# Rows 1 to 3 of a gated attention kernel: the input loaded already transposed, and normalized in that layout

## The chip, the cores and the metric

The kernel runs on one core of one Trainium2 chip. The metric is the device time of one execution in microseconds, the median of the runs: 1109.39 us over three runs (1108.53 to 1110.27) for the kernel before the change. The profile is one execution, recorded instruction by instruction. In what follows, PE or TensorE is the matrix engine, DVE is VectorE, ACT is ScalarE, POOL is GpSimd, and SP is the engine that here issues nearly all of the DMAs. L12 is line 12 of the kernel before.

## The reference

The input x has 4 rows of a batch, 512 tokens each, 1024 features. All of it is float32. Cut to what is computed:

```
xn  = (x - mean(x)) / sqrt(var(x) + 1e-5)              # per token, over the 1024 features
q, k, v = xn @ Wq, xn @ Wk, xn @ Wv                    # 16 heads of 64
q, k = rotary(q), rotary(k)
s   = softmax(causal(q k^T) / 8) v @ Wo
r   = softmax(xn @ gate_w.T)                           # 8 experts
g   = silu((xn * (r @ in_scale)) @ sign(weight).T * (r @ out_scale) + bias)
out = x + s * g
```

The normalization's mean and deviation belong to a token; everything that follows multiplies over features. On this chip a matmul sums over the partitions, so xn is needed with features on the partitions and tokens along the free dimension: transposed, against the way x lies in memory.

## The kernel before, in words

The code calls a row of the batch b (0 to 3). P is 128, E is 1024, S is 512 tokens of a row, NC = 8 is the number of feature chunks of 128, and TPB = 4 is the number of token tiles of 128 in a row. NGRP = 4 is the number of groups of four heads.

The first phase, up to about 800 us, goes through 16 stages (the loop over `groups`), a row's four quarters g = 0 to 3 one after the other. In each stage three kinds of work are woven together in 16 pieces (`interleave`):

- Projections of the current row (`projections`, `project_qk`, `project_v`, L338 and L425). Each product of two matrices is made by seven products of half size instead of eight, with sums of quarters of weights (S forms, `form_w`, L288) and of the input (T forms, `form_x`, L311 and, in the last row, L303). TensorE executes a float32 matmul as two instructions. Its results go through a ring of four PSUM banks of 128x512, and DVE and ACT read them out of it (L352, L358, L387, L389, L446, L451). The T forms of the next row are asked for at the end of a row's last quarter; the next row's first two products use X itself, the next ones T3 and T2.
- Attention of the group before (`attention_pieces`): scores on TensorE (L525), mask and maximum on DVE, exponential on ACT, scaling on POOL (`softmax`, L561), transposition of the probabilities in 32x32 blocks on DVE (`transpose_blocks`, L579) followed by 16 DMAs on SP that put the blocks in place (L589), and the product with the values (`values`, L604), copied out by ACT (L613) and stored to device memory (L617). Rotation (`rotary`) uses ACT (L319, L320), DVE (L321) and POOL (L322, L323).
- Preparation of the next row, which the change touches. In quarter g = 1 the first two token tiles of row b + 1 are loaded (`load_x`, L161) to two buffers. In quarters 2 and 3, two token tiles each: statistics by `layernorm_scales` (L171, L177, the square root on ACT L179), `normalize` (reciprocal L186, then one DVE instruction over 128 tokens x 1024 features, L187), then `transpose_x`: 8 TensorE transposes of 128x128 (L200) in two groups of four, each through one bank of the ring, the first group's bank copied to X by DVE (L204) and the second's by ACT (L206); then the tile of X is stored to device memory as `xn_d` (L210), from which the second phase loads it. The four groups of a stage stand at pieces 7, 8, 13 and 14.

Row 0 is prepared ahead of all this in a short stretch of its own, by the same functions. X has two buffers, so that X of the next row is filled while X of the current row is in use.

The last phase, from about 800 us on, makes the gated feed-forward product and the output projection. The change does not touch its code.

What sets the order: TensorE executes in the order of the program (`manual_schedule`). The order of the instructions on DVE, ACT and POOL and of the DMAs on SP is made when the program is built, by a scheduler that takes the program's order as priority and moves ahead what its own estimates say is ready; `keep_in_program_order` pins single instructions. On the chip each engine's queue is then strictly in that order, and an instruction that waits holds those behind it. Row 0's stretch is in program order on DVE and ACT too.

Of the kernel before, what the change touches and what calls it, by code (L numbers as in the profile page):

```python
# [9 lines left out]
F32 = mybir.dt.float32  # L10
F32R = mybir.dt.float32r
AF = mybir.ActivationFunctionType  # L12
ALU = mybir.AluOpType
# [7 lines left out]
B, S, E = 4, 512, 1024  # L21
H, D = 16, 64
NE = 8
P = 128
NT = B * S
NC = E // P
NPAIR = H // 2
NGRP = NPAIR // 2
TPB = S // P
# [13 lines left out]
def attn_gated_ffn_kernel(  # L43
    ctx: ExitStack,
    tc: tile.TileContext,
    x: bass.AP,
    wqk: bass.AP,
    wv: bass.AP,
    wo: bass.AP,
# [9 lines left out]
    nc = tc.nc  # L59
# [4 lines left out]
    st = ctx.enter_context(tc.tile_pool(name="stats", bufs=4))  # L64
    sgp = ctx.enter_context(tc.tile_pool(name="sign", bufs=1))
    dp = ctx.enter_context(tc.tile_pool(name="spill", bufs=1, space=DRAM))
# [6 lines left out]
        out=mask,  # L73
        in_=mask,
# [22 lines left out]
    for sign, base in ((1, 0), (-1, 7)):  # L97
        nc.gpsimd.affine_select(
            out=high,
            in_=high,  # L100
# [10 lines left out]
    xn_d = dp.tile([B, TPB, P, E], F32, name="xn_d")  # L111
    at_d = dp.tile([B, TPB, P, E], F32, name="at_d")

    rt_d = dp.tile([B, TPB, 32, P], F32, name="rt_d")

    sg = {n: sgp.tile([P, E], F32R, name=f"sg{n}") for n in range(NC - 1)}
# [4 lines left out]
    xp = ctx.enter_context(tc.tile_pool(name="xn", bufs=2))  # L121
# [26 lines left out]
    def tp_bank(name):  # L148
        return bank(name).rearrange("p (t q) -> p t q", t=TPB)


    X, xin = {}, {}
# [3 lines left out]
    def load_x(b, t):  # L156
        if b == 0:
            xt = X1[:, t, :]
        else:
            xt = xip.tile([P, E], F32, tag="x", name=f"x_{b}_{t}")  # L160
        nc.sync.dma_start(out=xt, in_=x[(b * TPB + t) * P : (b * TPB + t + 1) * P, :])  # L161
        xin[b, t] = xt

    BN, MV = {}, {}

    def half_statistics(b, t, j):
        if j == 0:
            BN[b, t] = st.tile([P, 2, 6], F32, tag="bn", name=f"bn_{b}_{t}")

        tc.keep_in_program_order(  # L170
            nc.vector.bn_stats(BN[b, t][:, j, :], xin[b, t][:, j * HALF : (j + 1) * HALF])  # L171
        )

    def deviation(b, t):
        stats = BN[b, t]
        mv = st.tile([P, 2], F32, tag="mv", name=f"mv_{b}_{t}")
        nc.vector.bn_aggr(mv, stats)  # L177
        std = st.tile([P, 1], F32, tag="std", name=f"std_{b}_{t}")
        nc.scalar.activation(std, mv[:, 1:2], AF.Sqrt, bias=eps)  # L179
        MV[b, t] = mv, std  # L180

    def normalize(b, t):
        xt = xin[b, t]
        mv, std = MV[b, t]
        rstd = st.tile([P, 1], F32, tag="rstd", name=f"rstd_{b}_{t}")
        nc.vector.reciprocal(rstd, std)  # L186
        nc.vector.tensor_scalar(xt, xt, mv[:, 0:1], rstd, op0=ALU.subtract, op1=ALU.mult)  # L187

    def layernorm_scales(b, t):
        half_statistics(b, t, 0)  # L190
        half_statistics(b, t, 1)
        deviation(b, t)

    def transpose_x(b, t, g):
        if b not in X:
            X[b] = xp.tile([P, NC, S], F32, tag="X", name=f"X_{b}")
        tp = tp_bank(f"xtp_{b}_{t}_{g}")
        for j in range(4):
            c = 4 * g + j
            nc.tensor.transpose(tp[:, j, :], xin[b, t][:, c * P : (c + 1) * P], ident)  # L200
        dst = X[b][:, 4 * g : 4 * g + 4, t * P : (t + 1) * P]

        if (g == 0 and b > 0) or (g == 1 and (b, t) == (0, TPB - 1)):
            nc.vector.tensor_copy(dst, tp)  # L204
        else:
            nc.scalar.copy(dst, tp)  # L206
        if g == 1:

            queue = nc.scalar if (b, t) == (B - 1, TPB - 1) else nc.sync
            queue.dma_start(  # L210
                out=xn_d[b, t].rearrange("p (c q) -> p c q", c=NC),
                in_=X[b][:, :, t * P : (t + 1) * P],
            )
# [469 lines left out]
    def load_scales(src):  # L683
        v = xip.tile([P, E], F32, tag="x", name="scales")
        nc.sync.dma_start(out=v, in_=src)
        scales.append(v)

    def split_scales(dst):
        v = scales.pop(0)
        h, low, sign = (row_kind[:, n : n + 1] for n in range(3))  # L690
        pin = tc.keep_in_program_order
        if not scales_done:
            pin(nc.vector.tensor_reduce(h, high, AX.X, ALU.max))
            pin(nc.vector.tensor_scalar(low, h, -1.0, 1.0, op0=ALU.mult, op1=ALU.add))
            pin(nc.vector.tensor_scalar(sign, h, 2.0, -1.0, op0=ALU.mult, op1=ALU.add))
        scales_done.append(dst)

        pin(nc.vector.tensor_copy(dst, v))
        pin(nc.vector.tensor_scalar(v, v, low, None, op0=ALU.mult))
        pin(  # L700
            nc.vector.scalar_tensor_tensor(
                dst, dst.bitcast(F32), sign, v, op0=ALU.mult, op1=ALU.add
            )
        )
# [141 lines left out]
    def attention_pieces(k, late):  # L846

        units = [(*groups[k], i) for i in range(2)]
        w, v = late
        u0, u1 = units  # L850

        def values_and_scores(before, u):
            def both():
                if before:
                    values(before)
                scores(u)
                softmax(u, 1, 3)

            return both

        pieces = [[] for _ in range(16)]

        last = k == len(groups) - 2
        plan = {
            2: lambda: v and transpose_blocks(v),
            3 if last else 4: values_and_scores(w, u0),
            4 if last else 6: lambda: softmax(u0, 2, 0),
            8 if last else 9: lambda: transpose_blocks(u0),  # L870
            9 if last else 12: values_and_scores(v, u1),
            10 if last else 14: lambda: softmax(u1, 2, 0),
        }
        if last:
            plan[14] = lambda: transpose_blocks(u1, ordered=True)
        for n, piece in plan.items():
            pieces[n].append(piece)
        return pieces, units
# [11 lines left out]
    for k, (b, g) in enumerate(groups):  # L890
        pieces = [[] for _ in range(9)]
        if k > 0:
            pieces, late = attention_pieces(k - 1, late)

        def at(n, piece):
            pieces[n].append(piece)


        if g == 0:
            routing = [lambda n=n: router(b, n) for n in range(3)]  # L900
            if k == 0:
                at(0, routing[0])
                at(1, lambda: (load_scales(in_scale), load_scales(out_scale)))
                at(2, routing[1])
                at(4, routing[2])
                at(5, lambda: split_scales(isc))
            else:
                if b < B - 1:
                    at(5, routing[0])
                at(8, routing[1])  # L910
                at(15, routing[2])
        elif g == 1 and b + 1 < B:

            at(11, lambda: [load_x(b + 1, t) for t in range(2)])
            if b == 0:
                at(1, lambda: split_scales(osc))
        elif g > 1 and b + 1 < B:
            t0 = 2 * (g - 2)

            layernorm_scales(b + 1, t0)  # L920
            layernorm_scales(b + 1, t0 + 1)
            normalize(b + 1, t0)
            at(3, lambda: normalize(b + 1, t0 + 1))
            for n, t, h in ((7, t0, 0), (8, t0, 1), (13, t0 + 1, 0), (14, t0 + 1, 1)):
                at(n, lambda t=t, h=h: transpose_x(b + 1, t, h))
            if g == 2:
                at(11, lambda: load_x(b + 1, 2))
                at(15, lambda: load_x(b + 1, 3))
        if k in (5, 9, 12, 14):
            n = {5: 0, 9: 2, 12: 4, 14: 6}[k]  # L930
            at(0, lambda: (load_sign(n), load_sign(n + 1)))
            at(8, lambda: make_sign(n))
            at(15, lambda: make_sign(n + 1))
        if b == B - 1:

            if g < 2:
                load_xn(g)
            if g in (1, 2):
                at(1, lambda: in_scales(g - 1, score_banks))
            if g == 3:  # L940
                z_place[0] = [xip.tile([P, E], F32, tag="x", name=f"z0_{i}") for i in range(2)]
                at(1, lambda: out_scales(0, score_banks))
        if k == 11:

            at(15, lambda: router(b + 1, 0))
        interleave(pieces, fill, 3 * 7 * 4 if k else 3 * 7 * 4 - 8)
        if g == NGRP - 1:
            for _ in fill:
                pass
            if b + 1 < B:  # L950
                for n in (3, 1, 2, 4) if b + 1 < B - 1 else (3, 2, 4, 1):
                    form_x(b + 1, n)
                fill = projections(b + 1)
# [98 lines left out]
    w, v = late  # L1052
# [374 lines left out]
```

## Time and profile before

| | |
|---|---|
| median of 3 runs | 1109.39 us (1108.53 to 1110.27) |
| span of the profiled execution | 1108.7 us; the page gives no other time for it, so it stands 0.7 us under the median |
| TensorE clock granted | 0.996 of full speed |
| DVE, ACT, POOL busy | 79%, 42%, 47% |
| transposes of x (L200) | 128, of which 96 are for rows 1 to 3 |
| DMA traffic | 163.88 MB, 109 GB/s of HBM over the span |
| row 0's projections begin | about 12 us |
| row 1's, 2's, 3's projections begin | about 194, 387 and 584 us |

How to read it: the busy share of TensorE counts each matmul from start to end though they overlap, so the cost of a TensorE step is read from the start times. A timeline line gives the start in us, the length in us, engine, line, operation, result <- operands, shape and count of merged instructions; in brackets, where there are any, the idle time before it and what ended it. A line of the table of stages gives the stretch, its length, the busy time of each engine with its number of instructions, the granted clock, the share of the DMA engines and GB/s.

### The profile page before, as it was taken

The numbers are of one execution on the slowest core, as the hardware profiler recorded it, in microseconds if no ns is written. First come the engines' busy times: TensorE is split into PE (matmuls) and PEld (weight loads), VectorE is DVE, ScalarE is ACT, GpSimd is POOL, SyncE is SP. The second block draws the span as 40 slices with busy tenths as digits, with TensorE's granted clock in tenths as the row PEclk, the third lists the DMA queues.
The fourth block names the chain that finished last, engine by engine and source line by source line (L and its number), as shares of the span: only waits on it lengthen the run. The fifth ranks groups of instructions, "written<-read, shape, count | busy, mean of one in ns | idle before, by whom it ended". The sixth has DMA issues, their size and how long they took to land. (4 is left out here: it accounts for less than half of the span.)

```text
span 1108.7 us, 15895 instructions
## 1 busy us (share of the span) xinstructions
PE 1087.4 (98%) x5176; PEld 790.2 (71%) x5176; DVE 870.4 (79%) x1740; ACT 461.3 (42%) x1072; POOL 518.9 (47%) x566
## 2 busy tenths in 40 slices
PE   9999999999999999999999999999999999999997
PEld 8887778777777877777788687777664545654663
DVE  7888888788988978888887887887776877567663
ACT  2452754453375445427544452655530223122220
POOL 0772645555264555526453562675552433432334
PEclk9999999999999999999999999999999999999999
DMA  9415566544556654455666445544664222431331
GB/s 323 135 69 147 149 184 189 160 137 119 166 155 187 190 154 135 121 163 158 184 183 219 140 148 142 153 125 122 179 193 171 90 93 102 148 119 54 136 114 57
DMA packets 86770, 163.88 MB, mean 148 GB/s; under 512 B 13472, under 2 KB 49056, under 8 KB 80672
## 3 DMA queue, kind: packets, MB, share of 16 engines
q1 hardware_dynamic: 80144, 152.25, 46.1%
q0 software_dynamic: 4832, 9.05, 2.4%
q10 hardware_dynamic: 1712, 1.57, 0.5%
q8 instruction: 41, 0.67, 0.3%
q14 instruction: 41, 0.34, 0.1%
HBM read 95.45 MB, written 25.43 MB: 109 GB/s over the span
## 5 line engine op out<-in xcount | busy, mean ns | idle before, releaser
L561 POOL TENSOR_SCALAR p<-p,rs 128x256 f32<-128x256 f32 (+3 forms) x256 | 183.7, 734 | 200.6 <-DVE rs L559 136.2
L551 ACT ACTIVATE p<-sc,nmx 128x256 f32<-128x256 f32 (+3 forms) x256 | 132.9, 529 | 104.8 <-DVE nmx L548 87.2
L338 PE MATMUL pj<-X,w 128*128 128x256 f32 x576 | 134.3, 382 | 1.7 <-ACT p L551 1.5
L338 PE MATMUL pj<-T,S 128*128 128x256 f32 x512 | 120.5, 385 | 8.5 <-ACT v L613 8.5
L579 DVE STREAM_TRANSPOSE y<-p 128x256 f32<-128x256 f32 x320 | 112.4, 409 | 18.3 <-POOL p L561 16.9
L322 POOL TENSOR_TENSOR sw<-sw,sin_sb 128x512 f32<-128x512 f32 x64 | 85.1, 1330 | 81.1 <-ACT sw L320 75.4
L338 PEld LDWEIGHTS pj<-X,w 128*128 128x128 f32 x576 | 108.1, 190 | 20.0 <-issue 2.9
L338 PEld LDWEIGHTS pj<-T,S 128*128 128x128 f32 x512 | 96.7, 192 | 24.8 <-ACT v L613 11.3
L319 ACT ACTIVATE sw<-c 32x512 f32<-32x512 f32 x128 | 80.3, 628 | 70.0 <-DVE c L352 68.2
L338 PE MATMUL pj<-T,w 128*128 128x256 f32 x448 | 106.6, 382 | 0.0
L548 DVE TENSOR_REDUCE nmx<-sc 128x1 f32<-128x256 f32 (+3 forms) x160 | 105.2, 683 | 1.3
L425 PE MATMUL pj<-w,X 128*128 128x256 f32 x416 | 94.6, 380 | 0.8 <-ACT p L551 0.5
L338 PEld LDWEIGHTS pj<-T,w 128*128 128x128 f32 x448 | 83.4, 190 | 15.5 <-issue 4.6
L323 POOL TENSOR_TENSOR rot<-rot,sw 128x512 f32<-128x512 f32 x64 | 90.8, 1419 | 5.0
L425 PEld LDWEIGHTS pj<-w,X 128*128 128x128 f32 x416 | 78.2, 190 | 12.7 <-ACT p L551 2.0
L545 DVE TENSOR_TENSOR sc<-sc,mask 128x256 f32<-128x256 f32 (+1 forms) x160 | 57.0, 371 | 35.3 <-PE sc L525 35.3
L320 ACT ACTIVATE sw<-c 32x512 f32<-32x512 f32 x128 | 80.4, 628 | 1.6
L425 PE MATMUL pj<-w,T 128*128 128x256 f32 x352 | 80.2, 381 | 0.0
L525 PE MATMUL sc<-rot,rot 64*128 64x128 f32 (+3 forms) x512 | 79.7, 443 | 0.3 <-DVE v L451 0.3
L604 PE MATMUL pv<-p,v 128*64 128x256 f32 (+3 forms) x512 | 76.0, 439 | 0.4 <-issue 0.4
L388 POOL TENSOR_TENSOR part<-part,part 128x256 f32<-128x256 f32 x32 | 24.7, 771 | 105.2 <-ACT part L387 102.0
L613 ACT COPY v<-pv 128x512 f32<-128x512 f32 x32 | 18.7, 585 | 131.5 <-PE pv L604 131.4
(177 smaller groups left out, 1956.9 us busy)
## 6 DMA issues: line engine op xcount, KB each, us to landing
p<-y SPq DMA_DIRECT2D x496, 80.0 KB, 2.1
w<-in_wqk SPq DMA_DIRECT2D x31, 1024.0 KB, 5.3
w<-in_wv SPq DMA_DIRECT2D x16, 1024.0 KB, 5.2
x<-in_x SPq DMA_DIRECT2D x16, 512.0 KB, 4.3
at_d<-v SPq DMA_DIRECT2D x32, 256.0 KB, 2.7
xp<-xn_d SPq DMA_DIRECT2D x16, 512.0 KB, 4.6
ap<-at_d SPq DMA_DIRECT2D x16, 512.0 KB, 5.1
xr<-in_x SPq DMA_DIRECT2D x32, 256.0 KB, 3.0
```

The lines of the kernel that those rows point to most:

```text
L319: nc.scalar.activation(sw[r : r + 32, :], c[r + 32 : r + 64, :], AF.Copy, scale=sc)
L320: nc.scalar.activation(sw[r + 32 : r + 64, :], c[r : r + 32, :], AF.Copy, scale=sc)
L322: nc.gpsimd.tensor_tensor(sw, sw, sin_sb, op=ALU.mult)
L323: nc.gpsimd.tensor_tensor(rot, rot, sw, op=ALU.add)
L338: nc.tensor.matmul(ps, lhsT=wq[:, k, :], rhs=xq[:, k, :], start=(k == 0), stop=(k == 3))
L425: nc.tensor.matmul(ps[:, j, :], lhsT=xq[:, k, j * P : (j + 1) * P], rhs=wq[:, k, :], start=(k == 0), stop=(k == 3),)
L525: nc.tensor.matmul(head(i, h), lhsT=Q[u][r : r + D, i * P : (i + 1) * P], rhs=K[u][r : r + D, : (i + 1) * P], start=True, stop=True,)
L548: nc.vector.tensor_reduce(nmx[:, hs], v, AX.X, ALU.max, negate=True)
L551: nc.scalar.activation(pt[:, h, :], ps[h], AF.Exp, bias=nmx[:, h : h + 1], accum_out=ssum[:, h : h + 1],)
L561: nc.gpsimd.tensor_scalar(pt[:, h, :], pt[:, h, :], rs[:, h : h + 1], 1.0, op0=ALU.mult, op1=ALU.mult,)
L579: nc.vector.transpose(out[:, :, :, o : o + 32], src.rearrange("p h (b c) -> p h b c", b=4))
L604: nc.tensor.matmul(by_block[r : r + D, :, 32 * j :], lhsT=V[u][:, j, r : r + D], rhs=PT[u][:, :, o : o + 32 * (TPB - j)], start=(j == 0), ...
```

## The change

A second copy of the input comes in, `xT`, laid out on the host with the features on the partitions: for each row, 128 partitions x (8 chunks x 512 tokens). For rows 1 to 3 it is loaded straight to X with four DMAs of 512 KB (`load_xT`, two at piece 9 and two at piece 15 of quarter 1). x itself is still loaded by token tiles for the statistics, but is no longer normalized nor transposed there. Instead, the mean and the reciprocal of the deviation of 128 tokens, two numbers on each partition, are written to a small tensor in device memory (`sv_d`, at the end of `layernorm_scales`) and read back as one line of 256 numbers broadcast to all partitions (`load_rows`, one buffer); then POOL subtracts the mean and DVE multiplies by the reciprocal, each as one instruction over 128 partitions x 8 chunks x 128 tokens, in place in X (`normalize_columns`), and the tile is stored to `xn_d` as before. The broadcast loads stand at pieces 3 and 9 of quarters 2 and 3, the normalizations at 6 and 12. Row 0 keeps the transposes; its code loses only the cases that were for the other rows. The store of row 3's last tile, which ACT's queue issued, goes to SP's.

```diff
+    sv_d = dp.tile([B, TPB, 2, P], F32, name="sv_d")
...
+    def load_xT(b, n):
+        if n == 0:
+            X[b] = xp.tile([P, NC, S], F32, tag="X", name=f"X_{b}")
+        for c in range(4 * n, 4 * n + 4, 2):
+            nc.sync.dma_start(
+                out=X[b][:, c : c + 2, :].rearrange("p c q -> p (c q)"),
+                in_=xT[b][:, c * S : (c + 2) * S],
+            )
+
     def layernorm_scales(b, t):
+
         half_statistics(b, t, 0)
         half_statistics(b, t, 1)
         deviation(b, t)
+        mv, std = MV[b, t]
+        nc.vector.reciprocal(mv[:, 1:2], std)
+        with nc.allow_non_contiguous_dma(reason="two numbers per token"):
+            nc.sync.dma_start(out=sv_d[b, t].rearrange("r p -> p r"), in_=mv)
+
+    ROW = {}
+
+    def load_rows(b, t):
+        ROW[b, t] = st.tile([P, 2, P], F32, tag="row", name=f"row_{b}_{t}", bufs=1)
+        nc.sync.dma_start(
+            out=ROW[b, t].rearrange("p r q -> p (r q)"),
+            in_=sv_d[b, t].rearrange("r q -> (r q)")[None, :].to_broadcast((P, 2 * P)),
+        )
+
+    def normalize_columns(b, t):
+        v = X[b][:, :, t * P : (t + 1) * P]
+        mean, rstd = (ROW[b, t][:, r, None, :].to_broadcast((P, NC, P)) for r in range(2))
+        nc.gpsimd.tensor_tensor(v, v, mean, op=ALU.subtract)
+        nc.vector.tensor_tensor(v, v, rstd, op=ALU.mult)
+        nc.sync.dma_start(out=xn_d[b, t].rearrange("p (c q) -> p c q", c=NC), in_=v)
...
         elif g == 1 and b + 1 < B:
 
+            at(9, lambda: load_xT(b + 1, 0))
             at(11, lambda: [load_x(b + 1, t) for t in range(2)])
+            at(15, lambda: load_xT(b + 1, 1))
...
             layernorm_scales(b + 1, t0)
             layernorm_scales(b + 1, t0 + 1)
-            normalize(b + 1, t0)
-            at(3, lambda: normalize(b + 1, t0 + 1))
-            for n, t, h in ((7, t0, 0), (8, t0, 1), (13, t0 + 1, 0), (14, t0 + 1, 1)):
-                at(n, lambda t=t, h=h: transpose_x(b + 1, t, h))
+            for n, t in ((3, t0), (9, t0 + 1)):
+                at(n, lambda t=t: load_rows(b + 1, t))
+                at(n + 3, lambda t=t: normalize_columns(b + 1, t))
```

More of the change, by code (lines that the diff above doesn't have):

```diff
@@ L46, in attn_gated_ffn_kernel @@
     x: bass.AP,
+    xT: bass.AP,
     wqk: bass.AP,
@@ L201, in transpose_x @@
         dst = X[b][:, 4 * g : 4 * g + 4, t * P : (t + 1) * P]
-        if (g == 0 and b > 0) or (g == 1 and (b, t) == (0, TPB - 1)):
+        if g == 1 and t == TPB - 1:
             nc.vector.tensor_copy(dst, tp)
@@ L207, in transpose_x @@
         if g == 1:
-            queue = nc.scalar if (b, t) == (B - 1, TPB - 1) else nc.sync
-            queue.dma_start(
+            nc.sync.dma_start(
                 out=xn_d[b, t].rearrange("p (c q) -> p c q", c=NC),
@@ L1405 @@
         "x": np.ascontiguousarray(a["hidden_states"].reshape(NT, E)),
+        "xT": np.ascontiguousarray(
+            a["hidden_states"].reshape(B, S, NC, P).transpose(0, 3, 2, 1).reshape(B, P, NC * S)
+        ),
         "wqk": np.ascontiguousarray(np.stack([by_group(a["Wq"]), by_group(a["Wk"])], axis=1)),
```

## The prediction

> **What bounds the kernel now.** I read the page's busy row first, then the TensorE timeline around the step that goes, then the busy table of the six stages that hold it (the last two quarters of rows 0, 1 and 2), then the DVE, POOL and SP timelines of one of them.
>
> ```profile
> PE 1087.4 (98%) x5176; PEld 790.2 (71%) x5176; DVE 870.4 (79%) x1740; ACT 461.3 (42%) x1072; POOL 518.9 (47%) x566
> ```
>
> TensorE is never out of work: of 21.3 us without a matmul, 1.5 lie before the first one and most of the rest after the last. But a busy matmul is a pipelined one (382 ns long, started every 216 ns), so what a step costs is read from the starts in the timeline:
>
> ```profile
> 186.31 0.60 PE L200 MATMUL xtp<-ident,x 128*128 128x128 f32 x4
> 186.75 2.32 PE L425 MATMUL pj<-w,T 128*128 128x256 f32 x10
> 188.91 0.60 PE L200 MATMUL xtp<-ident,x 128*128 128x128 f32 x4
> 189.34 1.03 PE L425 MATMUL pj<-w,T 128*128 128x256 f32 x4
> 190.21 3.62 PE L425 MATMUL pj<-w,X 128*128 128x256 f32 x16
> 193.66 3.62 PE L338 MATMUL pj<-X,w 128*128 128x256 f32 x16
> 197.12 3.62 PE L338 MATMUL pj<-T,S 128*128 128x256 f32 x16
> ```
>
> Four transposes hold the engine from 186.31 to 186.75, so 0.44 us, with matmuls close before and behind them. They are not in a hole; without them the rest moves up.
>
> ```profile
> 145.00:193.60 48.60, 48.12 (x250) 38.06 (x249) 43.46 (x91) 25.87 (x60) 24.09 (x26) 1.00 0.61 179
> 340.00:387.20 47.20, 47.06 (x246) 37.10 (x245) 42.05 (x89) 25.86 (x60) 22.92 (x24) 1.00 0.60 178
> 533.00:583.50 50.50, 50.36 (x315) 39.80 (x314) 43.61 (x92) 26.14 (x61) 25.86 (x29) 1.00 0.62 178
> ```
>
> The columns are the length, then PE, weight loads, DVE, ACT, POOL, clock, DMA share, GB/s. In these stages DVE is the second engine, at 86 to 89%; ACT and POOL have half their time free, DMA a third. So TensorE sets the end, and DVE is what a gain can run into.
>
> **What goes.** Rows 1 to 3 have 12 tiles of 128 tokens, 8 transposes each: 24 groups of four, each 0.436 or 0.437 us from its first start to the next matmul's, 10.48 us together, all on the path. With them go 12 DVE copies (L204, 0.68 us) and 12 ACT copies (L206, 0.59), 8.1 and 7.0 us, and 24 uses of the four ring banks. ACT and the banks were not the bound; I cost that relief at nothing, though three stalls of 1.20, 1.38 and 1.39 us (TensorE waiting for ACT's v copy, L613) could shrink: at most 4 us below the sum.
>
> **DVE.** Out go 12 normalizations (L187, 10.9 us in all, mean 0.91) and the copies: 19.0 us. In come 12 multiplies of 128x1024 with two SBUF inputs. The nearest row is the T form (L311), the same size and kind: 1.22 to 1.64 us, so 14.6 to 19.7 us. The reciprocal stays (0.15). The balance is -4.4 to +0.7 us; the statistics (L171) are untouched.
>
> **POOL.** 12 subtractions of 128x1024 are new. POOL's tensor_tensor takes 0.75 to 0.77 us at 256 columns and 1.33 to 1.42 at 512, so 2.2 to 2.5 ns a column: 2.5 to 2.7 us at 1024, some 31 us in all. POOL has the room (it stands idle 7.0 us before 164.14 and 9.7 before 187.37), but a longer POOL instruction can hold DVE:
>
> ```profile
> 150.71 0.76 DVE L187 TENSOR_SCALAR x<-x,mv,rstd 128x1024 f32<-128x1024 f32 x1
> ...
> 154.40 1.58 DVE L187 TENSOR_SCALAR x<-x,mv,rstd 128x1024 f32<-128x1024 f32 x1
> ```
> ```profile
> 154.16 1.27 POOL L322 TENSOR_TENSOR sw<-sw,sin_sb 128x512 f32<-128x512 f32 x1 [0.20 <-DVE rstd L186]
> ```
>
> The same instruction took 0.76 us and, begun inside a POOL instruction that ended at 155.43, 1.58: it ended 0.55 us after POOL did, most of its own length later. The weight forms (L288, 128x512) likewise go from 0.69 to as much as 1.64. [...] By the rows alone, DVE reads PSUM or transposes in between (L352, L579 show no such growth), and meets POOL at a random point of the subtraction: 0 to 2.6 us a tile, 1.3 in the middle, 16 us in all. The six stages hold 298.3 us with 255.1 of DVE; with 10.5 us of length gone and 12 to 16 more work DVE would be at 93 to 94%. It still fits, but with little left.
>
> How much of DVE's lateness reaches TensorE? Up to 800 us DVE loses some 30 us to POOL (its SBUF instructions against their shortest), and TensorE's stalls there sum to about 10: at most a third. A third of 16 us is 5, none is 0; I take the middle, 2.5 us, because product banks are four deep, with 1.7 to 3.5 us a product.
>
> **The new chain.** Statistics (four DVE half tiles), ACT's square root, reciprocal, a DMA of mean and deviation to device memory, a broadcast load, subtraction, multiply, store. In the trace's third-quarter stage the reciprocals are done at 150.4 and 154.2. The two small DMAs have no row. The write (256 pieces of 4 bytes) lies between the router's 16 KB write (1.5 us to land) and the gate weights' 32 KB in 1024 pieces of 32 bytes (9.0, amid the start's rush); I take 3, nearer the first in size and hour. The load (128 KB) is nearest to the routing load of 32 KB (2.2) and the 256 KB loads (3.0): 2.6. [...] The first tile is then done about 154 + 6 + 2.6 + 1.4 = 164, the second some 8 us later, as one row buffer serves both. Needed: by the T forms, now at 190.03. Off the path by 15 us or more. Behind the subtraction that waits for its row stand, on POOL, the softmax scalings (L561, on which DVE's transposes wait) and the rotations; behind the multiply that waits for POOL, on DVE, the evacuations (L352, L451), on which TensorE's banks wait. The code leaves three pieces, some 9 us, from broadcast to subtraction against 2.6 for the load, so I cost these waits at nothing beyond the 2.5 above; a row late by more is rival 1.
>
> SP issues 12 more DMAs a row (four loads of 512 KB, four writes, four broadcasts), 0.3 to 0.6 us each, some 6 us a row of 193 us; 6 MB on top of 164 over DMA engines a third idle. The loads go to a buffer that has been free for most of a row: nothing. What queues behind the waiting broadcast on SP is a run of 16 p moves (L589), the attention stores and weight loads; the p moves issued at 154.18 are used at 178.95, so a 3 us wait is covered; without that cover it would be 3 us a stage. The store of row 3's last tile moves from ACT's queue to SP's; it now lands so late that DVE stands 4.7 us at L311, without a TensorE stall.
>
> **Sum.** Profiled span 1108.7 (the page gives no other time for that execution, and it is 0.7 under the median of 1109.39). 1108.7 - 10.5 + 2.5 = 1100.7, plus the 0.7 to the median: 1101.4.
>
> **Rival 1: the row comes late, slower.** SP's runs of p moves are long:
>
> ```profile
> 120.03 0.33 SPq L161 DMA_DIRECT2D x<-in_x  x1
> 124.30 0.59 SPq L210 DMA_DIRECT2D xn_d<-X  x1
> 128.30 10.90 SPq L589 DMA_DIRECT2D p<-y  x16
> ...
> 175.94 10.92 SPq L589 DMA_DIRECT2D p<-y  x16
> 186.96 0.53 SPq L617 DMA_DIRECT2D at_d<-v  x1
> ```
>
> The code places the second broadcast of a stage behind such a run. If it is issued there, at 186.96, the row lands at 189.6; POOL has up to 7.0 us of softmax work from 190.56; with subtraction and multiply X is whole at 194 to 201, against 190.1 now. The T forms (T3, T1, T2: 5.5 us with what lies between) then end at 199 to 206, and T2 is wanted at 198.8, less the 1.7 us gained in the stage: a stall of 2 to 9 us at each of three row boundaries. After a stall of 2.34 us TensorE's next 16 matmuls took 5.41 us instead of 3.62, so 1.8 more each time. It decides from 3.5 us a boundary; at 4 plus 1.8 it costs 17: 1116. Against it: the x load at 120.03 stands in the code behind the p moves of 128.30 and was issued first, so what is ready overtakes. 0.20.
>
> **Rival 2: DVE becomes the bound.** [...] For it: 86 to 89% of DVE, and ACT's v copy already late behind DVE. Against it: DVE's idle 43 us there. 0.16.
>
> **Rival 3: more than the transposes.** The three v stalls go too, and X is ready earlier, so the T forms leave DVE's crowded end of a row: 1095 to 1098. 0.10. That the transposes stay is excluded: the calls are gone.
>
> **How the numbers follow.** Forecast 0.54 (1098 to 1105), rivals 0.20, 0.16, 0.10. Range 1097 to 1112: it drops rival 1's heavier part and half of rival 3. This kernel's measurement tells 0.2%, 2.2 us, from no change. Faster: 0.54 + 0.10 + 0.05 of rival 2 + 0.01 of rival 1 = 0.70; same: 0.06 of rival 2 + 0.02 of rival 1 = 0.08; slower: 0.17 of rival 1 + 0.05 of rival 2 = 0.22.
>
> **What would show it.** L200 with 32 matmuls instead of 128; TensorE's gaps in the six stages near 6 us as now, or 2 to 3 more; subtractions of 2.5 to 2.7 us and multiplies of 1.2 to 1.6 (longer: lock); the multiply of a row's last tile ended before 190 in row 0's clock. Rival 1 would show a stall of TensorE behind L311 at each row boundary and broadcasts right after p moves; rival 2 stalls behind DVE's L352, L451 or ACT's L613. I am wrong if DVE stands in front of the multiply waiting for POOL by more than 2 us a tile.

## The result, and the profile after

The changed kernel takes 1162.48 us (median of 4 runs, 1160.16 to 1165.21), against 1108.96 for the kernel before (four runs). The ratio is 1.048, 95% interval 1.046 to 1.050: 53.5 us slower, where 8 us faster was predicted. The profiled execution has a span of 1158.2 us. Lines of the kernel after differ from those of before; the subtraction is L222, the multiply L223, the write L208, the broadcast load L214, the p moves L619.

The page's busy row, each engine with its share of the span:

```profile
PE 1089.2 (94%) x5080; PEld 789.3 (68%) x5080; DVE 879.6 (76%) x1728; ACT 454.8 (39%) x1060; POOL 547.5 (47%) x578
```

DVE has 9 us more to do than before and a lower share of the span (76% for 79%); POOL has 29 us more and the same share (47%). No engine became the bound: TensorE waits, for work that is waiting itself. The table of the three last quarters (length; PE, weight loads, DVE, ACT, POOL; clock; DMA share; GB/s), cut at the same work as before:

```profile
152.00:211.70 59.70, 48.47 (x234) 37.90 (x233) 44.88 (x90) 24.54 (x58) 27.31 (x26) 0.89 0.55 141
362.60:423.30 60.70, 48.59 (x234) 37.95 (x233) 45.56 (x91) 24.91 (x61) 27.78 (x27) 0.89 0.70 150
573.00:635.00 62.00, 54.28 (x317) 42.69 (x316) 49.76 (x96) 26.03 (x64) 32.14 (x33) 0.94 0.65 171
```

The stages of 48.6, 47.2 and 50.5 us became 59.7, 60.7 and 62.0. TensorE is idle for 11 and 12 us in the first two, and the granted clock fell from 1.00 to 0.89 there. The TensorE timeline of the first, with one line of the stage ahead of it:

```profile
118.87 5.93 PE L368 MATMUL pj<-X,w 128*128 128x256 f32 x16 [5.05 <-ACT p L581]
...
167.26 1.89 PE L368 MATMUL pj<-X,S 128*128 128x256 f32 x8
180.37 9.36 PE L455 MATMUL pj<-w,X 128*128 128x256 f32 x32 [11.23 <-ACT p L581]
189.57 3.62 PE L455 MATMUL pj<-S,T 128*128 128x256 f32 x16
```

One such stall stands in each of the six stages: 5.05, 11.23, 7.96, 12.11, 6.65 and 6.20 us, 49.2 together, as two lines of the table of waits have it (waiter and releaser: us in total, times, longest):

```profile
PE pj L455 <- ACT p L581: 29.5, 3, 12.1
PE pj L368 <- ACT p L581: 19.7, 3, 8.0
```

Each is followed by matmuls at half pace, one started every 427 ns instead of every 216: 16 took 5.13 to 5.96 us instead of 3.62, so 1.5 to 2.3 us more, 12 in all. 49.2 + 12 less the 10.5 of the transposes is 51, near the 53.5 us between the medians and the 49.5 between the two profiled spans.

Whom does ACT's exponential wait for? ACT's timeline ends an idle 14.26 us with DVE's maxima; then DVE's and POOL's timelines of the same stretch, and SP's:

```profile
178.46 1.28 ACT L581 ACT_TABLE_LOAD   x1 [14.26 <-DVE nmx L578]
```
```profile
163.87 1.96 DVE L318 TENSOR_TENSOR w<-w 128x1024 f32<-128x1024 f32 x1
175.84 1.23 DVE L223 TENSOR_TENSOR X<-X,row 128x1024 f32<-128x1024 f32 x1 [10.01 <-DMA p<-y]
176.98 0.95 DVE L575 TENSOR_TENSOR sc<-sc,mask 128x256 f32<-128x256 f32 x3
```
```profile
162.61 2.13 POOL L353 TENSOR_TENSOR rot<-rot,sw 128x512 f32<-128x512 f32 x1
173.46 2.34 POOL L222 TENSOR_TENSOR X<-X,row 128x1024 f32<-128x1024 f32 x1 [8.72 <-DMA p<-y]
```
```profile
156.32 0.38 SPq L208 DMA_DIRECT2D sv_d<-mv  x1
159.48 0.38 SPq L208 DMA_DIRECT2D sv_d<-mv  x1
165.19 0.33 SPq L214 DMA_DIRECT2D row<-sv_d  x1
165.62 13.83 SPq L619 DMA_DIRECT2D p<-y  x16
```

The scores were ready by 165.9, and DVE was free from 165.8. But the next instruction in DVE's queue is the multiply. It waits for POOL's subtraction, that for the row, and the row's load was issued at 165.19, when the first write had landed, 8.9 us after 156.32. The row landed 8.2 us later. The releaser "p<-y" of POOL's line is only the last DMA that ended there; the one that it needed is the row. Behind the multiply stand masks and maxima, behind those ACT's exponential, and behind that the banks that TensorE wants (two of the score tiles lie in the ring that the products use).

The whole kernel, from the table of waits, and from the groups of L208 and L214 the time from issue to landing:

```profile
POOL X L222 <- DMA row<-sv_d: 48.6, 4, 16.2
POOL X L222 <- DMA p<-y: 17.4, 2, 8.7
DVE X L223 <- POOL X L222: 25.5, 4, 7.1
DVE X L223 <- DMA p<-y: 20.0, 2, 10.0
```
```profile
L208 SPq DMA_DIRECT2D sv_d<-mv x12: 365/377/378, 97.8 to 582.3; - x12
...
DMA to landing us min/median/max: 7.2/8.9/13.8
```
```profile
L214 SPq DMA_DIRECT2D row<-sv_d x12: 320/473/655, 108.2 to 600.9; - x12
...
DMA to landing us min/median/max: 3.5/6.8/8.2
```

DVE stands in front of the multiply six times of twelve, once a stage, for 45.5 us in all; TensorE's stalls are 49.2.

### The profile page after: what moved, and what is told of

It reads as the page before. It is cut to its first block, busy times and chain, and to the rows that moved or that the text cites. A ratio compares the mean times of both kernels' runs of the same rounds, so it can differ in the third digit from the quotient of the medians.

```text
span 1158.2 us, 15764 instructions
## 1 busy us (share of the span) xinstructions
PE 1089.2 (94%) x5080; PEld 789.3 (68%) x5080; DVE 879.6 (76%) x1728; ACT 454.8 (39%) x1060; POOL 547.5 (47%) x578
## 3 DMA queue, kind: packets, MB, share of 16 engines
q1 hardware_dynamic: 87904, 160.66, 48.6%
## 5 line engine op out<-in xcount | busy, mean ns | idle before, releaser
L591 POOL TENSOR_SCALAR p<-p,rs 128x256 f32<-128x256 f32 (+3 forms) x256 | 180.7, 723 | 162.4 <-DVE rs L589 130.7
L368 PE MATMUL pj<-X,w 128*128 128x256 f32 x576 | 140.1, 394 | 19.9 <-ACT p L581 19.7
L368 PEld LDWEIGHTS pj<-X,w 128*128 128x128 f32 x576 | 112.1, 197 | 40.1 <-ACT p L581 20.9
L455 PE MATMUL pj<-w,X 128*128 128x256 f32 x416 | 99.6, 398 | 31.1 <-ACT p L581 29.5
L455 PEld LDWEIGHTS pj<-w,X 128*128 128x128 f32 x416 | 82.7, 200 | 45.5 <-ACT p L581 30.7
L575 DVE TENSOR_TENSOR sc<-sc,mask 128x256 f32<-128x256 f32 (+1 forms) x160 | 55.9, 369 | 25.1 <-PE sc L555 25.0
L455 PEld LDWEIGHTS pj<-w,T 128*128 128x128 f32 x352 | 66.4, 190 | 10.8 <-issue 2.0
```

Source lines behind the costliest of these rows:

```text
L368: nc.tensor.matmul(ps, lhsT=wq[:, k, :], rhs=xq[:, k, :], start=(k == 0), stop=(k == 3))
L455: nc.tensor.matmul(ps[:, j, :], lhsT=xq[:, k, j * P : (j + 1) * P], rhs=wq[:, k, :], start=(k == 0), stop=(k == 3),)
L591: nc.gpsimd.tensor_scalar(pt[:, h, :], pt[:, h, :], rs[:, h : h + 1], 1.0, op0=ALU.mult, op1=ALU.mult,)
```

## The experiments

Times are set against the kernel before in runs on the same chip, so "+10.1 us" is a median less that kernel's median there; in brackets stand the median, the ratio and its 95% interval. The changed kernel stands at +53.5.

The theory: **A**, DVE stands in front of a multiply whose row is still under way. The rivals: **A2**, the small DMAs harm by themselves; **B**, DVE and POOL hold each other up, the expectations' "lock" (in the kernel before, DVE's L187 took 0.76 us, and 1.58 when begun inside POOL's L322; that took 1.27, and 1.75 when begun inside L187); **C and D**, the multiply, or the subtraction, costs its own length on its engine.

### The row from a constant table, without and with the write left out (e1, e2)

```diff
-            in_=sv_d[b, t].rearrange("r q -> (r q)")[None, :].to_broadcast((P, 2 * P)),
+            in_=cos[0:1, 0 : 2 * P].to_broadcast((P, 2 * P)),
```

> The broadcast rows are read from the cosine table instead of from the tensor of means and deviations, so the normalization uses wrong numbers and its load waits for no write; the 4-byte writes, the loads, subtractions and multiplies stay. Theory A (the multiply stands at the head of DVE until the write and the row have landed): the wait goes, near 1100 to 1110 us. Theory B (the subtractions and multiplies themselves, by lock and by work, hold DVE): still 1150 to 1160. If the 4-byte writes hold up the other DMAs enough to matter by themselves, it stays above 1115.

> As the run with constant rows, and the 4-byte writes are left out too. Theory A: 1098 to 1104 us, the transposes' 10.5 us less a little. Theory B: 1150 to 1160. The difference to the run with the writes is what the writes cost by themselves: 0 to 3 us if only their waiters lose, 5 or more if they hold up other transfers.

Measured: +42.5 us (1152.73, ratio 1.038, 1.035 to 1.042) and +24.6 us (1134.81, 1.022, 1.019 to 1.025). Neither isolates what it was made for. With nothing to wait for, the scheduler put the subtractions right behind the row loads in earlier stages; in the second run they still waited 32.6 us for rows (up to 10.5). Taking away a dependency also changes the order, and with it the place of the wait.

### Pieces of 8 bytes instead of 4 (e3)

```diff
-    sv_d = dp.tile([B, TPB, 2, P], F32, name="sv_d")
+    sv_d = dp.tile([B, TPB, P, 2], F32, name="sv_d")
...
-            nc.sync.dma_start(out=sv_d[b, t].rearrange("r p -> p r"), in_=mv)
+        nc.sync.dma_start(out=sv_d[b, t], in_=mv)
```

> Mean and reciprocal lie side by side in device memory: 128 writes of 8 bytes instead of 256 of 4, and the row is read with a stride of two. If the landing of the write (8.9 us) goes with the number of pieces, it falls to 4 to 6 us and the time by 12 to 25 us, to 1137 to 1150; if it is a fixed cost of a DMA to device memory or a queue of other transfers, landing and time stay (1155 to 1165). Theory B: no change.

Measured: +26.1 us (1136.34, 1.024, 1.020 to 1.027). The write now lands in 6.0 us instead of 8.9 (4.4 to 7.5), TensorE's stalls behind the exponential fell from 49.2 to 22.6 us (`PE pj L454 <- ACT p` 11.9, `PE pj L367 <- ACT p` 10.7). The same two engine instructions, an earlier row, half the loss: against C and D as the whole. SP's waits for the writes shrank with it (11.0 us in six for 31.3), so it does not tell A from A2.

### The kernel before with the writes alone (e4)

```diff
+        mv, std = MV[b, t]
+        with nc.allow_non_contiguous_dma(reason="two numbers per token"):
+            nc.sync.dma_start(out=sv_d[b, t].rearrange("r p -> p r"), in_=mv)
```

> The kernel before, with the 12 writes of 256 pieces of 4 bytes added (mean and variance to device memory) and nothing that reads them: the writes' cost by themselves. Theory A1 (only who waits for a write loses): 1109 to 1111 us. Theory A2 (a write also holds the DMA engines, so that transfers behind it land late): 1115 to 1130, with the p moves and weight loads behind it landing several us late.

Measured: -1.4 us (1109.03, 0.9986, 0.9972 to 1.0000). Twelve writes that nothing reads cost nothing, though SP's table of waits puts 12.8 us in five waits down to them. The page's packet count shows what a write is: packets under 512 B rose from 13472 to 16736, so 272 for each write of 256 numbers, 16 more than one a number.

### No normalization at all, and then the small DMAs alone (e6, e16)

```diff
-        nc.gpsimd.tensor_tensor(v, v, mean, op=ALU.subtract)
-        nc.vector.tensor_tensor(v, v, rstd, op=ALU.mult)
```

The first of the two also drops the write and the row load; the second keeps both.

> The changed kernel without mean and deviation in rows 1 to 3 (no write, no row, no subtraction, no multiply: x enters as it is): the transposes' place alone. Theory A: 1097 to 1100 us, the 10.5 us of the transposes. If it stays above 1105, the loads of the transposed input or the order of the rest cost something, and neither the rows nor the normalization is the whole cause.

> The changed kernel without its subtraction and multiply: the 12 writes of 256 pieces of 4 bytes and the 12 broadcast row loads stay where they were, and nothing reads the rows (x enters the products as it is). Theory A (the loss is engine instructions standing in front of rows under way): 1097 to 1102 us, like the kernel without the DMAs (1097.8). Rival A2 (the small DMAs delay the p moves and the weight loads by themselves): 1110 us or more, with TensorE waiting for the weights or the p moves.

Measured: without normalization -12.6 us (1097.79, 0.989, 0.986 to 0.991); with the small DMAs +2.0 us (1111.24, 1.002, 1.001 to 1.004). So write and row load cost 14.6 us though nothing reads the rows, and A's 1097 to 1102 is a miss. (1.5 of the 14.6 arise at a stall of 2.34 us that both kernels have, at 610.20 and 623.34 us: the 16 matmuls behind it took 3.72 us in the one and 5.41 in the other.) SP's timeline without the DMAs, with them, and DVE's line there:

```profile
153.66 10.99 SPq L614 DMA_DIRECT2D p<-y  x16
```
```profile
152.45 0.38 SPq L208 DMA_DIRECT2D sv_d<-mv  x1
158.02 0.33 SPq L214 DMA_DIRECT2D row<-sv_d  x1
158.45 13.83 SPq L616 DMA_DIRECT2D p<-y  x16
```
```profile
174.62 0.45 DVE L606 STREAM_TRANSPOSE y<-p 128x256 f32<-128x256 f32 x1 [4.25 <-DMA p<-y]
```

The row load waits on SP for its write, and the 16 p moves stand behind it: issued from 158.45 instead of 153.66, over 13.83 us instead of 10.99. Then DVE stands 4.25 us in front of a transposition and TensorE waits for DVE's sums of the products for v (8.4 us in four stalls, the first of which, 1.1 us, is there without the DMAs too). The writes alone cost nothing in the kernel before, which points at the load: its wait on SP (33.1 us in six waits, by the table of waits) or its traffic. The two were not tried apart, and e4's waits (12.8 us at -1.4) show that a wait on SP need not cost anything.

### Rows without device memory: who does the work (e8, e9, e10)

TensorE transposes the mean and the deviation, each read 128 times over, into a PSUM bank; ACT copies it to the row buffer. Rows at pieces 4 and 8, steps at 5 and 9.

```diff
+        tp = bank(f"svp_{b}_{t}")[:, : 2 * P].rearrange("p (r q) -> p r q", r=2)
+        for r in range(2):
+            nc.tensor.transpose(tp[:, r, :], mv[:, r : r + 1].to_broadcast((P, P)), ident)
+        nc.scalar.copy(ROW[b, t], tp)
```

e8 keeps POOL's subtraction and DVE's multiply; e9 gives both to POOL, e10 both to DVE.

> The result of the reference, without device memory: TensorE transposes each number's column, read as 128 equal columns, so that mean and reciprocal come out spread over the partitions (two instructions, 0.22 us a tile), and ACT copies them out (0.4 us); subtraction and multiply as in the change. Theory A: no stalls in front of the multiply, 1109.4 - 10.5 + 2.6 = 1101.5, so 1100 to 1107 us. Theory B: 1140 or more.

> As the run without device memory (1120.5 us), with both subtraction and multiply on POOL; the result is the reference's. That run lies 22.7 us above the one without normalization (1097.8), of which 2.6 are TensorE's 24 small transposes. Theory C (the 20 us are DVE's 12 multiplies, each of which stands or runs in front of evacuations): 1100 to 1108 us. Theory D (they are POOL's instructions, which lock DVE or come in front of the softmax scalings): 1120 or more, since POOL's work doubles.

> As the run without device memory, with both subtraction and multiply on DVE, so that DVE never waits for POOL there and POOL has nothing new. The result is the reference's. Theory C: DVE has 15 us more work, 1125 to 1140. Theory D: 1105 to 1115, for the lock and POOL's queue are gone.

Measured: e8 +10.1 us (1120.46, 1.009, 1.006 to 1.012), e9 +29.9 (1139.52, 1.027, 1.024 to 1.030), e10 +4.1 (1113.71, 1.004, 1.003 to 1.006). The trip through memory goes and with it 43 of the 53.5 us (the pieces at which the steps are asked for moved too, by one to three); 1120.5 lies between the ranges of A and B. e9 and e10 both fell in D's ranges: more work for POOL was dearer here than more work for DVE, though POOL is busy for only 47% of the changed kernel. In e9 DVE waits 25.1 us for POOL's part sums, 12.5 in the kernel before. The small transposes cost TensorE 0.22 to 0.27 us a tile by the starts in the timeline, some 3 us.

### Two lines of 512 bytes to memory (e7)

```diff
+        nc.tensor.transpose(tp, MV[b, t][0], ident)
+        nc.scalar.copy(two, tp)
+        nc.sync.dma_start(out=sv_d[b, t], in_=two)
```

> The result of the reference: the two numbers of a tile are transposed by TensorE (one instruction of 0.11 us) and written to device memory as two lines of 512 bytes, then broadcast as before. Theory A: the write lands in 1.5 to 3 us instead of 8.9, the stall in front of the first multiply falls to 0 to 3 us a stage: 1102 to 1118 us. Theory B (work and lock of subtraction and multiply): 1145 or more.

The writes stand at pieces 3 and 4, the loads at 4 and 9, the steps three later. Measured: +30.5 us (1140.86, 1.027, 1.024 to 1.030). The trace has no landing for these writes, so the 1.5 to 3 us are neither confirmed nor refuted; of the row loads it has two, 3.7 and 5.2 us. POOL waits little for rows now, and DVE still waits for POOL:

```profile
POOL X L227 <- DMA row<-sv_d: 6.2, 4, 3.5
DVE X L228 <- POOL X L227: 27.4, 9, 5.7
```

The stalls moved: 13.1 us stand behind ACT's copy of v in three third quarters, and 15.4 at the rows' ends, over half of it in this line:

```profile
PE lg L664 <- DVE X L228: 8.2, 1, 8.2
```

That is rival 1's place: the next row's first product (here the router's) behind the last tile's multiply. So with hardly a late row left, the version still loses 30.5 us; the late row is not all of it.

### Steps pinned later; the statistics a stage ahead (e5, e11, e12, e17)

```diff
-            for n, t in ((3, t0), (9, t0 + 1)):
-                at(n, lambda t=t: load_rows(b + 1, t))
-                at(n + 3, lambda t=t: normalize_columns(b + 1, t))
+            for n, t in ((9, t0), (13, t0 + 1)):
+                at(3, lambda t=t: load_rows(b + 1, t))
+                at(n, lambda t=t: normalize_columns(b + 1, t))
```

This is e5, with both steps under `keep_in_program_order` and two row buffers. e12 is e5 with rows from the constant table; e11 is e8 pinned at 5 and 13; e17 puts statistics, writes and row loads one quarter ahead of the steps, unpinned.

> The result of the reference: both rows of a stage are loaded as soon as they are written (two buffers that lie idle until the last row), and subtraction and multiply are held in program order at pieces 9 and 13, so that DVE passes the softmax maxima before it comes to the first multiply. Theory A: the stalls of 5 to 12 us in front of the first multiply go, 1100 to 1110 us, though write and row land as late as before. Theory B: 1150 or more.

> As the run without device memory, with subtraction and multiply held in program order, the first tile's at piece 5, the second's at piece 13, away from the transposes of probabilities and the evacuations of pieces 9 to 12. The result is the reference's. If the stalls of 3.7 us in the third quarters came from the second tile's multiply before those evacuations, they fall to the 1 to 1.7 us of the run without normalization, and the time to 1106 to 1113. If they are DVE's load in general, 1118 or more.

> As the run with pinned order and device memory (1155.1 us), with the rows read from the cosine table, so that no row waits for a write and SP waits for none (the normalization uses wrong numbers); writes, loads, subtractions and multiplies stay, in the same pinned places. Theory A (the trip through device memory, by waits on SP, POOL and DVE): 1105 to 1122, as the run without device memory or a little better. If the normalization in these places costs that much by itself, 1145 or more.

> The changed kernel with its 4-byte writes and broadcast loads kept, but statistics, write and row load one quarter (about 48 us) ahead of the subtraction and the multiply, two row buffers, and the loads of x one quarter earlier. Theory A (the loss is DVE standing in front of a multiply whose row is still under way): no subtraction waits for a row, and the time is that of the run without device memory, 1114 to 1124 us. Rival A2 (the small DMAs cost by themselves, by holding the p moves and the weight loads): 1135 us or more, with the subtractions waiting for nothing.

Measured: e5 +44.9 us (1155.12, 1.041, 1.037 to 1.044), e11 +24.4 (1134.08, 1.022, 1.019 to 1.025), e12 +34.6 (1144.28, 1.032, 1.026 to 1.038), e17 +62.4 (1172.31, 1.055, 1.053 to 1.058). All missed their better case. A late step is not a free one: pinned, DVE waits 28.7 us (e5) and 34.3 us (e11, without memory) for POOL's subtraction, and the last tile reaches the row's boundary. e12 differs from e5 in the source of the rows alone: in that pinned order, rows that wait for no write are worth some 10 us (44.9 less 34.6, two runs each). In e17 the steps moved ahead with their rows, in POOL's and DVE's timelines:

```profile
73.03 2.34 POOL L222 TENSOR_TENSOR X<-X,row 128x1024 f32<-128x1024 f32 x1 [6.52 <-DMA row<-sv_d]
```
```profile
75.40 1.23 DVE L223 TENSOR_TENSOR X<-X,row 128x1024 f32<-128x1024 f32 x1 [9.68 <-POOL X L222]
```

The stall is of the same kind as in the changed kernel, a stage earlier (TensorE stands 12.18 us before 79.95). That run did not take the wait away, so it does not decide between A and A2.

### Place, and the row read from PSUM (e13, e14, e15, e18)

e13 is e10 with rows at 3 and 5 and steps at 4 and 6; e15 is e13 with POOL's subtraction. e14 is e13 and e18 is e10, each without ACT's copy: DVE reads the row in PSUM.

```diff
-        ROW[b, t] = rtp.tile([P, 2, P], F32, tag="rt", name=f"row_{b}_{t}")
-        nc.scalar.copy(ROW[b, t], tp)
+        ROW[b, t] = tp
```

> The kernel with rows spread by TensorE and both steps on DVE (1113.7 us) with its places moved ahead: rows at pieces 3 and 5, steps at 4 and 6. Theory 'place' (what is left above 1097.8 + 2.6 us comes from where the two steps of some 1.3 us each stand among the product copies and maxima): the stall of 1.86 us per stage goes, 1104 to 1109 us. Theory 'work' (12 x 2 more DVE instructions of 1.3 us in stages where DVE is at about 90% cost the same wherever they stand): 1112 to 1115.

> As the run before it, but DVE reads the rows from the PSUM bank where TensorE left them, without a copy by ACT: the two steps then have one SBUF input instead of two. Theory 'lock' (DVE loses to POOL in instructions with two SBUF inputs): the two steps stay at 1.2 to 1.3 us each and the time falls by 3 to 6 us against the run before. Theory 'no lock': within 2 us of it, or 2 to 5 us slower, since the bank, one of four, stays taken until the second step has ended.

> As the first run of this batch, but the subtraction on POOL as in the change. Theory 'POOL's subtraction costs its length': 6 to 8 us above the first run (as 1120.5 stands to 1113.7 at the later places), with DVE idle in front of the multiply. Rival: at the earlier places POOL is free, and it comes within 2 us of the first run.

> The kernel with rows read by DVE from PSUM (1112.4 us with rows at pieces 3 and 5) at the places of the first kernel without memory: rows at 4 and 8, steps at 5 and 9. The two ways to spread the rows by ACT's copy measured 1125.4 at 3 and 5 and 1113.7 at 4 and 8, so 11.7 us by place; the copy and the second SBUF input cost 13.0 at 3 and 5. If the two add up, 1100 to 1104 us, faster than before. If they are the same stalls (ACT's v copy standing behind the row copy), 1109 to 1113.

Measured: e13 +15.5 us (1125.39, 1.015, 1.013 to 1.016): earlier is dearer, not cheaper, a miss for both readings. e15 +26.6 (1136.50, 1.024, 1.022 to 1.025): POOL's subtraction costs 11 us more than DVE's. e14 +2.4 (1112.35, 1.002, 1.001 to 1.003), e18 -2.2 (1107.12, ratio 0.9982, 0.9973 to 0.9991). The copy and the SBUF row cost 13.0 us at the early places, 6.2 at the later ones; 1107.1 lies between the two ranges, so neither reading held. TensorE's timeline of the same step in e13 and e14 shows where the early places lost it:

```profile
137.45 3.72 PE L367 MATMUL pj<-T,S 128*128 128x256 f32 x16 [2.86 <-ACT v L642]
```
```profile
136.03 3.72 PE L366 MATMUL pj<-T,S 128*128 128x256 f32 x16 [0.94 <-ACT v L641]
```

DVE's two steps take 1.22 and 1.25 us in e13, 1.22 and 1.21 in e14 (medians; 30.9 and 29.2 us in all), so the loss is not their own length. Whether it is ACT's copy or what POOL and DVE lose to each other was not separated. e18 is the one version of the change that gives the reference's result and is faster than before, by 0.18%, at the edge of what the measurement can tell. It stands 10.4 us above no normalization: some 3 us of small transposes, and 9.8 us of stalls in the six stages against 3.7 there.

## Why the prediction was wrong, point by point

- **The transposes**: right. -10.5 us were predicted, and the kernel without normalization is 12.6 faster; it also lost DVE's normalizations and the copies, and what those 2 us are was not tried.
- **The sizes of the two steps**: right, or nearly: 2.35 us for the subtraction where 2.5 to 2.7 were said, 1.22 for the multiply at the low end of 1.22 to 1.64. From the groups of L222 and L223 (min/median/max in ns):

```profile
L222 POOL TENSOR_TENSOR X<-X,row x12: 2339/2350/2802, 112.0 to 612.6; 128x1024 f32<-128x1024 f32 x12
```
```profile
L223 DVE TENSOR_TENSOR X<-X,row x12: 1210/1224/2296, 114.3 to 617.9; 128x1024 f32<-128x1024 f32 x12
```

- **The price of what they displace**: too low. 2.5 us for POOL and DVE together; without memory the two steps and the spreading cost 22.7 us (+10.1 against -12.6), and 16.7 with both on DVE. What DVE loses to POOL was sized well: DVE is busy 879.6 us, 850.8 without normalization, and the 12 multiplies are 15.7 of the difference, so 13.1 us remain where 16 were said. DVE's busy share said there was room, and the two steps cost far more than the 5 us that were the upper bound. How much of the 22.7 is DVE's loss to POOL was not separated.
- **The small DMAs**: mis-sized. "I take 3" and 2.6 became 8.9 and 6.8 (medians). The upper bound of the write, 9.0, was the 1024 pieces of 32 bytes, the row nearest in kind; I took the row nearest in bytes. The load's bounds, 2.2 to 3.0, did not hold it at all.
- **"Needed: by the T forms, now at 190.03. Off the path by 15 us or more"**: the step that failed. It asks when the data is used, and puts the waits on the way there at nothing. They measured 45.5 us of DVE standing in front of the multiply and 49.2 us of TensorE's stalls. The queue needs the multiply when it comes to the head of DVE's queue, at 165.8, and everything behind it then waits. The prediction named what stands there, and cost it at nothing because "the code leaves three pieces, some 9 us, from broadcast to subtraction". The order is made by the scheduler, by its own estimates of landings, and those pieces were gone: POOL was free for the subtraction at 164.7, the row's load went out at 165.19.
- **SP**: "a 3 us wait is covered; without that cover it would be 3 us a stage". The waits for the writes were 5.5 us on average (33.1 in six, e16), and with them write and load cost 14.6 us for six stages with nothing reading the rows, 2.4 a stage.
- **Rival 1**, a row that comes late, had the mechanism at 0.20 but put it at the row boundary behind the p moves, 4 + 1.8 us three times. It came at the first tile of each of six stages, 8.2 + 2 us each. In the changed kernel the second broadcast went out at 181.46, ahead of the p moves, as the argument against the rival said.
- **Its own test**: "I am wrong if DVE stands in front of the multiply waiting for POOL by more than 2 us a tile". It stood 45.5 us for 12 tiles, 3.8 each.

What adds up, and what doesn't: from -12.6 us, 14.6 for the DMAs, 22.7 for the work without memory, and 28.8 that remain, which only the combination shows. I read them as engine instructions waiting for rows. The sum assumes that the three add. That e3's earlier row halves the loss, and that the six DVE waits match the six stalls, support the reading. Against taking it as a price stand e7, which loses 30.5 us with hardly a late row, and e12, which gains only some 10 us on e5. No version has rows that wait for nothing in the changed kernel's own order, so the 28.8 is a remainder, not a measurement.

## What to carry to other kernels

An instruction with a late input is due when it comes to the head of its queue, not when its output is wanted (here 45.5 us of DVE in front of the multiply, 49.2 of TensorE behind it); look up who is behind it, and price the wait there. Do not take the distance in the source for the distance in the queue where a scheduler orders the engines. Here, small numbers that must change from partitions to rows went cheaper through TensorE and PSUM than through device memory (+10.1 us against +53.5), and cheapest with both steps on DVE and the rows read from PSUM where they are (-2.2).

## What the runs showed of the hardware

- Time from issue to landing of a small write to device memory fell with the number of pieces: 256 of 4 bytes 8.9 us (7.2 to 13.8), 128 of 8 bytes 6.0 (4.4 to 7.5), medians of 12 each, in the changed kernel and in e3. A broadcast of 1 KB to 128 partitions took 6.8 us (3.5 to 8.2) in the changed kernel and 5.1 (3.5 to 10.0) in e16, with nothing reading it.
- TensorE's pace after a stall: half (a matmul started every 427 ns instead of every 216) for 3.0 to 4.4 us after each of the six stalls of 5 to 12 us. After a stall of 1.86 us in e10 it was full twice and half once (16 matmuls in 3.72, 3.72 and 5.38 us); after one of 2.86 us in e13 it was full (3.72). The length of the stall alone did not decide it here.
